# Depthwise 3x3 convolutions of a vision model: from nine diagonal matmuls to three stacked-row matmuls per 32-channel strip

## The chip, the cores and the metric

The kernel runs on one core of one Trainium2 chip. The metric is the device time of one execution in microseconds (us), the median of three runs. The engines are called PE (TensorE), DVE (VectorE), ACT (ScalarE), POOL (GpSimd) and SP (SyncE, which here only issues DMAs).

## The reference

The input is `x`, 8 images of 56x56 pixels and 192 channels, in f32. Four residual layers follow one another, each on the group-normalized (32 groups) result of the one before:

```python
x = x + L0(gn(x))   # gated Toeplitz mixing along rows and columns, 576 inner channels
x = x + L1(gn(x))   # shifted 7x7 window attention, 6 heads
x = x + L2(gn(x))   # depthwise 3x3 convolution, 192 channels, zero padding, bias
x = x + L3(gn(x))   # in_proj to 2x384, depthwise 3x3 convolution of 384 channels, SiLU,
                    # selective scans of 16 states in 4 directions, layer norm, gate, out_proj
```

A depthwise convolution treats every channel by itself: output pixel (h, w) of channel c is the sum over dy, dx of w[dy, dx, c] times the pixel (h+dy-1, w+dx-1) of the same channel, with zeros outside the image. The change concerns the two depthwise convolutions, in L2 (called conv2 below) and in L3 (conv3).

## The kernel before, in words

Channels lie on the partitions, pixels along the free axis, and an image is taken in seven chunks of 8 rows (448 pixels, `CH`). The program has three phases.

1. `products` and `toeplitz` for images 0 to 3 (layer L0's mixing).
2. The `front` of image 0, and between its pieces `products` and `toeplitz` of images 4 to 7. What is left of these when the front is done is run after it. A scheduler of the framework orders this phase.
3. The scans of all eight images, and between them the fronts of images 1 to 7. The order of this phase is written out by the kernel itself.

`front(b)` is a chain of five stages: `gate` (L0's end), `attention` (L1), `conv2` (L2), `inner` (in_proj and conv3 of L3), `steps` (the scan's coefficients). Each is a Python generator that yields between pieces of work. All of them work in one SBUF buffer, `slab`, which each stage carves up anew.

The scan goes over 224 chunks (8 images, 4 directions, 7 chunks), each with 3 channel blocks `d` and 8 pairs of states `k`: 5376 steps. One step multiplies on POOL (`ring`, L1007), exponentiates on ACT (L1024), scans on DVE (L1033), multiplies by C on POOL or DVE in turn (`hc`, L1039), and adds up on PE with two matmuls by the identity (`ps_y`, L1054). `hc` has four buffers. SP loads `bm` and `cm`, broadcast rows, some eight steps ahead.

In the loop over the steps a planner (`Parts`) keeps a modelled clock for each engine. After each step it lets the front run on as long as the modelled work fits before the next scans; the costs come from `Meter`, which gives a PE instruction 0.04 us plus 1.25 ns a column. The order that results is fixed when the program is built, and each engine runs its list in order. A front must have made a chunk's coefficients before that chunk's scan comes up, else the planner runs the front alone until it has.

conv2 before: for each chunk `load_x` brings 10 rows of each 96-channel half (one row above and below), DVE normalizes them into a tile `xp` with a zero column at each side (L736), and nine matmuls add the nine taps (L749). Each has a 96x96 diagonal matrix of one tap as its weights (made once, kept in DRAM as `dg2_d`) and a shifted view of `xp` as moving data. DVE adds bias and residual (L758) and takes statistics. After each three matmuls the generator yields.

conv3 before: for each of the three 128-channel blocks, in_proj writes its convolution half into a padded image `xp` in SBUF (58x58, L804) and the other half through `zt`, two buffers, to `zr_d` in DRAM (L801, L802). Then for each chunk nine matmuls with 128x128 diagonals (`dg3_d`) follow (L817), and ACT evicts (L826). SiLU, and a transposed copy, follow for the whole block, with stores of 1.5 MB each.

The front of image 0 and the first closing passage of a scan (`finish`, which norms, gates and projects) run through a metering helper, so their instructions have line L79 in the profile. (L0 to L3 above are layers; elsewhere L and a number is a line of the kernel.)

Of the kernel before, what the change touches and what calls it, by code (L numbers as in the profile page):

```python
# [38 lines left out]
SLAB, SLAB_F = 10048, 2688 + HALF  # L39
SLOT = NG * (CH + 1) + HALF  # L40
# [18 lines left out]
class MeteredEngine:  # L59
# [3 lines left out]
    def __getattr__(self, name):  # L63
# [3 lines left out]
        def call(*args, **kw):  # L67
            n, extra = 0, 0.0
            for v in list(args) + list(kw.values()):
                if hasattr(v, "shape") and (engine != "E" or n == 0):  # L70
                    m = 1
                    for s in v.shape[1:]:
                        m *= s
                    n = max(n, m)
            if name == "preload_act_table_set" or AF.Silu in args or AF.Softplus in args:
                extra = 1.28
            if name != "dma_start":
                self.meter.log.append((engine, base + each * n + extra))
            return f(*args, **kw)  # L79
# [5 lines left out]
def model(ctx: ExitStack, tc: tile.TileContext, a: dict, out: bass.AP):  # L85
# [31 lines left out]
    dg2_d = dram.tile([CP, 2, 9, CP], F32, name="dg2_d")  # L117
    dg3_d = dram.tile([128, ND, 9, 128], F32, name="dg3_d")
# [178 lines left out]
    with (  # L297
# [66 lines left out]
        cw2, cw3, dg2, dg3 = carve(slab, 128, (2, 9), (ND, 9), (2, 9, CP), (ND, 9, 128))  # L364
        nc.sync.dma_start(out=cw2[:CP], in_=a["cw2"])
        nc.sync.dma_start(out=cw3, in_=a["cw3"])
        for t in range(9):
            for k in range(2):
                nc.vector.tensor_scalar_mul(dg2[:CP, k, t, :], ident[:CP, :CP], cw2[:CP, k, t : t + 1])
            for d in range(ND):  # L370
                nc.vector.tensor_scalar_mul(dg3[:, d, t, :], ident, cw3[:, d, t : t + 1])
        nc.sync.dma_start(out=dg2_d, in_=dg2[:CP])
        nc.sync.dma_start(out=dg3_d, in_=dg3)
# [316 lines left out]
        def conv2(b):  # L690

            dg, xh, xp, xo = carve(slab, CP, (2, 9, CP), (2, 2, 10, W), (2, 2, 10, W + 2), (2, 2, CH))
            nc.sync.dma_start(out=dg, in_=dg2_d)

            def span(j):

                return max(8 * j - 1, 0), min(8 * j + 9, H)

            def load_x(j):
                r0, r1 = span(j)  # L700
                at = r0 - (8 * j - 1)
                for k in range(2):
                    nc.sync.dma_start(
                        out=xh[:, j % 2, k, at : at + r1 - r0, :],
                        in_=x2_d[b][k * CP : (k + 1) * CP, r0 * W : r1 * W].rearrange("p (h w) -> p h w", w=W),
                    )


            def load_all(j):
                nc.sync.dma_start(out=xo[:, j % 2], in_=blocks(x2_d[b])[:, :, j * CH : (j + 1) * CH])  # L710

            load_all(0)
            load_all(1)
            yield 0, 0, 6.0
            for j in range(NCH):
                for k in range(2):
                    nc.vector.bn_stats(out=st[:, k, j, :], in_=xo[:, j % 2, k, :])
                    yield 0, 0, 2.0
                if j + 2 < NCH:
                    load_all(j + 2)  # L720
            load_x(0)
            yield from group_norm(NCH)
            for u in range(2):
                for k in range(2):
                    nc.scalar.activation(xp[:, u, k, :, 0 : W + 2 : W + 1], ident[:CP, 0:20].rearrange("p (h u) -> p h u", u=2), AF.Copy, scale=0.0)
            nc.scalar.activation(xp[:, 0, :, 0, :], ident[:CP, : 2 * W + 4].rearrange("p (k w) -> p k w", k=2), AF.Copy, scale=0.0)
            for j in range(NCH):
                r0, r1 = span(j)
                at = r0 - (8 * j - 1)
                u = j % 2  # L730
                if j + 1 < NCH:
                    load_x(j + 1)
                else:
                    nc.scalar.activation(xp[:, u, :, 9, :], ident[:CP, : 2 * W + 4].rearrange("p (k w) -> p k w", k=2), AF.Copy, scale=0.0)
                for k in range(2):
                    nc.vector.tensor_scalar(  # L736
                        xp[:, u, k, at : at + r1 - r0, 1 : W + 1],
                        xh[:, u, k, at : at + r1 - r0, :],
                        mr[:, k, 0:1],
                        mr[:, k, 1:2],  # L740
                        ALU.subtract,
                        ALU.mult,
                    )
                for k in range(2):
                    yield 0, 1
                    p = bank()
                    for t in range(9):
                        dy, dx = divmod(t, 3)
                        nc.tensor.matmul(  # L749
                            p[:CP, :CH],  # L750
                            dg[:, k, t, :],
                            xp[:, u, k, dy : dy + 8, dx : dx + W],
                            start=t == 0,
                            stop=t == 8,
                        )
                        if t % 3 == 2:
                            yield 1, 0
                    nc.vector.scalar_tensor_tensor(  # L758
                        xo[:, u, k, :],
                        p[:CP, :CH],  # L760
                        cb2[:, k : k + 1],
                        xh[:, u, k, 1:9, :].rearrange("p h w -> p (h w)"),
                        ALU.add,
                        ALU.add,
                    )
                    nc.vector.bn_stats(out=st[:, k, j, :], in_=xo[:, u, k, :])
                nc.sync.dma_start(out=blocks(x3_d[b])[:, :, j * CH : (j + 1) * CH], in_=xo[:, u])
# [3 lines left out]
        def inner(b):  # L771

            w_in, x, zt, xp, xc = carve(slab, 128, (2, 2 * 128), (2, 2, CH), (2, CH), (H + 2, W + 2), (L,))
            dg = carve(slab[:, 512:], 128, (9, 128))[0]
            w_in, x = w_in[:CP], x[:CP]
            for d in range(ND):
# [10 lines left out]
                for e in (xp[:, 0 : H + 2 : H + 1, :], xp[:, :, 0 : W + 2 : W + 1]):  # L787
                    nc.scalar.activation(e, ident[:, :116].rearrange("p (u v) -> p u v", u=e.shape[1]), AF.Copy, scale=0.0)
                for j in range(NCH):
                    if j + 1 < NCH:  # L790
                        load_x(j + 1)
                    for u in range(2):
# [7 lines left out]
                        if u:  # L800
                            nc.scalar.activation(zt[:, j % 2, :], p[:, :CH], AF.Identity, bias=nb[:, 1:2])  # L801
                            nc.sync.dma_start(out=zr_d[b][:, d, j * CH : (j + 1) * CH], in_=zt[:, j % 2, :])  # L802
                        else:
                            nc.scalar.activation(  # L804
                                xp[:, 8 * j + 1 : 8 * j + 9, 1 : W + 1],
# [4 lines left out]
                nc.sync.dma_start(out=dg, in_=dg3_d[:, d])  # L810
                yield 0, 0, 6.0
                for j in range(NCH):
                    yield 0, 1
                    p = bank()
                    for t in range(9):
                        dy, dx = divmod(t, 3)
                        nc.tensor.matmul(  # L817
                            p[:, :CH],
                            dg[:, t, :],
                            xp[:, 8 * j + dy : 8 * j + dy + 8, dx : dx + W],  # L820
                            start=t == 0,
                            stop=t == 8,
# [547 lines left out]
```

## Time and profile before

| what | value |
|---|---|
| median of three runs | 21839.35 us (21826.98 to 21850.64) |
| the profiled execution, its own time | 21800.17 us |
| its span | 21798.4 us, 194536 instructions |
| PE, DVE, ACT, POOL busy | 84%, 73%, 56%, 69% of the span |
| conv2's matmuls (L749, images 1 to 7) | 1764 instructions, 725.1 us busy |
| conv3's matmuls (L817, images 1 to 7) | 2646 instructions, 1086.4 us busy |
| the scan's adding matmuls (L1054) | 21504 instructions, 9818.6 us busy |
| DMA | 3249.8 MB, mean 149 GB/s |

Busy shares are averages over three phases with different limits: POOL does next to nothing in the first 3.4 ms. An f32 matmul appears as two instructions. A group's mean is the time of one instruction from start to end, and neighbours overlap on PE, so busy time divided by the count says what one costs in a dense stretch.

### The profile page before, as it was taken

Reading aid. Unit: us, or ns where it says so; the run is one execution under the profiler, and the core shown is the slowest. Engines: PE = TensorE matmul, PEld = TensorE weight load, DVE = VectorE, ACT = ScalarE, POOL = GpSimd, SP = SyncE. Lnnn points to the kernel's source line nnn. Section 1 sums busy time; section 2 is a strip of 40 time slices with the busy share of each in tenths; the row PEclk is TensorE's granted clock in tenths of the full one; section 3 lists DMA queues with packets and bytes.
Section 4 is the critical chain, followed back from the end, with each engine's and each line's share of the span. In section 5 each row is a group of like instructions: output and inputs, shape, how many; then the busy total and the mean of one; then the engine's idle time right before and its main releaser. Section 6 shows DMA issues by size and latency. Waiting matters only on the chain. (4 is left out here: it accounts for less than half of the span.)

```text
span 21798.4 us, 194536 instructions
## 1 busy us (share of the span) xinstructions
PE 18274.4 (84%) x58396; PEld 9706.4 (45%) x58396; DVE 15858.5 (73%) x12604; ACT 12098.2 (56%) x28153; POOL 15084.9 (69%) x9175
## 2 busy tenths in 40 slices
PE   7978977888888989888888889888988888887777
PEld 4845654444443434444444434443444444343333
DVE  2122117996799768986799769976898589976998
ACT  3126114655666466755666566746675566656555
POOL 0000006887789778977788768976898678877998
PEclk9588868999999989998999989998999899998888
DMA  3931575444544455445644455345544464445443
GB/s 86 245 98 49 170 196 169 126 135 159 187 143 135 136 184 170 129 129 171 184 133 136 154 184 150 123 150 170 169 129 140 156 185 132 135 155 175 134 138 116
DMA packets 2419572, 3249.82 MB, mean 149 GB/s; under 512 B 917598, under 2 KB 2361024, under 8 KB 2387554
## 3 DMA queue, kind: packets, MB, share of 16 engines
q1 hardware_dynamic: 2398292, 3121.12, 47.5%
q0 software_dynamic: 15520, 116.14, 1.4%
q8 instruction: 463, 7.59, 0.1%
q14 instruction: 593, 4.86, 0.1%
q10 hardware_dynamic: 4704, 0.12, 0.0%
HBM read 2661.35 MB, written 575.48 MB: 148 GB/s over the span
## 5 line engine op out<-in xcount | busy, mean ns | idle before, releaser
L1007 POOL TENSOR_TENSOR ring<-du,bm 128x896 f32<-128x896 f32 x5376 | 9447.8, 1771 | 1983.9 <-ACT ring L1014 1937.8
L1054 PE MATMUL ps_y<-hc,ident_sb 128*128 128x448 f32 x21504 | 9818.6, 591 | 590.2 <-POOL hc L1039 573.3
L1024 ACT ACTIVATE ps_a<-delta,A_logs_sb 128x449 f32<-128x449 f32 x10752 | 6858.4, 638 | 331.5 <-DVE ring L1033 68.7
L1054 PEld LDWEIGHTS ps_y<-hc,ident_sb 128*128 128x128 f32 x21504 | 4271.5, 207 | 4640.8 <-issue 3494.9
L1033 DVE TENSOR_TENSOR_SCAN ps_a<-ps_a,ring 128x898 f32<-128x898 f32 x2688 | 5429.0, 2020 | 1062.5 <-ACT ring L1014 555.0
L1033 DVE TENSOR_TENSOR_SCAN ring<-ps_a,ring 128x898 f32<-128x898 f32 x2688 | 5423.0, 2017 | 420.4 <-ACT state L1046 177.3
L1039 POOL TENSOR_TENSOR hc<-ring,cm 128x896 f32<-128x896 f32 x2688 | 4758.0, 1770 | 860.9 <-DVE ring L1033 349.3
L1039 DVE TENSOR_TENSOR hc<-ps_a,cm 128x896 f32<-128x896 f32 x2688 | 2935.0, 1092 | 974.5 <-PE ps_y L1054 753.3
L1046 ACT COPY state<-ps_a 128x2 f32<-128x2 f32 x2687 | 425.3, 158 | 3254.0 <-DVE hc L1039 3250.0
L280 DVE COPY tzx<-ps_tz 112x448 f32<-112x448 f32 x432 | 269.8, 625 | 1389.9 <-PE ps_tz L274 1175.0
L274 PE MATMUL ps_tz<-tzx,tm 112*112 112x112 f32 x4608 | 1031.5, 403 | 257.6 <-DMA tm<-ext 233.0
L288 POOL DMA_DIRECT2D o<-tzx x192 | 97.3, 513 | 1653.6 <-DVE tzx L280 1318.7
L274 PEld LDWEIGHTS ps_tz<-tzx,tm 112*112 112x112 f32 x4608 | 1028.0, 319 | 295.2 <-issue 288.7
L817 PE MATMUL ps_f<-slab 128*128 128x448 f32 x2646 | 1086.4, 546 | 69.9 <-DMA slab<-dg_d 62.1
L1046 ACT COPY state<-ring 128x2 f32<-128x2 f32 x2688 | 504.9, 188 | 791.3 <-DVE ring L1033 778.4
L647 PE MATMUL ps_f<-ident_sb,slab 98*98 98x98 f32 x1344 | 336.5, 326 | 619.6 <-ACT slab L640 619.6
L749 PE MATMUL ps_f<-slab 96*96 96x448 f32 x1764 | 725.1, 547 | 47.7 <-DVE slab L736 47.7
L817 PEld LDWEIGHTS ps_f<-slab 128*128 128x128 f32 x2646 | 506.8, 192 | 560.5 <-issue 485.0
L79 PE MATMUL ps_f<-slab 96*96 96x448 f32 (+6 forms) x2306 | 731.2, 497 | 10.2 <-DMA slab<-x 4.9
L990 POOL TENSOR_TENSOR du<-delta,xcd 128x448 f32<-128x448 f32 x672 | 658.6, 980 | 23.6 <-DMA xcd<-xc 23.6
L647 PEld LDWEIGHTS ps_f<-ident_sb,slab 98*98 98x98 f32 x1344 | 203.9, 158 | 1033.7 <-ACT slab L640 814.6
L227 PE MATMUL ps_qv<-wqv,xn 96*128 96x384 f32 (+1 forms) x1200 | 527.0, 522 | 128.2 <-DVE xn L146 67.5
(218 smaller groups left out, 17070.7 us busy)
## 6 DMA issues: line engine op xcount, KB each, us to landing
bm<-bc SPq DMA_DIRECT2D x1792, 448.0 KB
cm<-bc SPq DMA_DIRECT2D x1792, 448.0 KB
xcd<-xc SPq DMA_DIRECT2D x840, 224.0 KB
dl<-slab SPq DMA_DIRECT2D x224, 672.0 KB
delta<-dl SPq DMA_DIRECT2D x224, 672.0 KB
tzx<-qv SPq DMA_DIRECT2D x192, 588.0 KB
o<-tzx POOLq DMA_DIRECT2D x192, 588.0 KB, 13.7
slab<-x SPq DMA_DIRECT2D x224, 336.0 KB
```

The lines of the kernel that those rows point to most:

```text
L79: return f(*args, **kw)
L274: nc.tensor.matmul(po[:, c, :], t[:, :, c2 + c], x[:, :, c1 + c2 + c], start=True, stop=True)
L647: nc.tensor.transpose(p[:PT_, e * PT_ : (e + 1) * PT_], S[:, 3 * g + e, :], ident[:PT_, :PT_])
L749: nc.tensor.matmul(p[:CP, :CH], dg[:, k, t, :], xp[:, u, k, dy : dy + 8, dx : dx + W], start=t == 0, stop=t == 8,)
L817: nc.tensor.matmul(p[:, :CH], dg[:, t, :], xp[:, 8 * j + dy : 8 * j + dy + 8, dx : dx + W], start=t == 0, stop=t == 8,)
L990: nc.gpsimd.tensor_mul(du[:, 0, :], deltas[i][:, d, 1 : CH + 1], xcs.pop((i, d)))
L1007: nc.gpsimd.tensor_mul(hs[:, :, tokens(i)[0]], dus[i, d].to_broadcast([128, NG, CH]), bms[i, k])
L1024: nc.scalar.activation(dA[:, n, :], deltas[i][:, d, at : at + CH + 1], AF.Exp, scale=negA[:, slot, d, c : c + 1])
L1033: nc.vector.tensor_tensor_scan(h, dA, hs, 0.0, ALU.mult, ALU.add)
L1039: (nc.gpsimd if on_pool(d, k) else nc.vector).tensor_mul(hc, h[:, :, tokens(i)[0]], cms[i, k])
L1046: nc.scalar.copy(states[i][:, d, NG * k : NG * k + NG], h[:, :, tokens(i)[2]])
L1054: nc.tensor.matmul(yps[i, d][:, :CH], ident, hcs[g][:, n, :], start=k + n == 0, stop=k + n == NP + NG - 2)
```

## The change

The convolution over dy moves into the contraction. Three copies of 32 channels, shifted by 0, 1 and 2 image rows, lie one above the other on 96 partitions. The weights of one dx are then a 96x32 matrix (three 32x32 diagonals), and one matmul yields 32 channels; three matmuls (dx) make up one 32-channel strip. A strip's output goes to its own 32 PSUM partitions[...]. A chunk takes 3 strips x 3 = 9 matmuls for a 96-channel half in conv2 as before, and 4 x 3 = 12 instead of 9 for a 128-channel block in conv3. All matmuls of a chunk are issued before the generator yields.

The shifted copies are made by DMA. The normalized input (conv2) and in_proj's output (conv3) are stored with a zero column at each side into padded images in DRAM (58x58, two for each convolution, used by images in turn); for each group three DMAs, one for each dy, load the rows from there into `xs`, two buffers. The top and bottom rows of the padded images are set to zero once, by ten DMAs on ACT's queue. In conv2 the normalization moves from DVE to ACT, the input is loaded once, without the neighbouring rows, into four buffers `xh`, and each loaded chunk is also the residual and the place of the result. In `inner` the padded image in SBUF is gone; `zt` has one buffer instead of two. The planner's model counts a matmul into 32 columns or fewer at a third of its columns.

```diff
+            if engine == "E" and args[0].shape[0] <= 32:
+                n /= 3
...
-    dg2_d = dram.tile([CP, 2, 9, CP], F32, name="dg2_d")
-    dg3_d = dram.tile([128, ND, 9, 128], F32, name="dg3_d")
+    dg2_d = dram.tile([CP, C // 32, 3, 32], F32, name="dg2_d")
+    dg3_d = dram.tile([CP, DI // 32, 3, 32], F32, name="dg3_d")
+    pad2_d, pad3_d = (
+        [dram.tile([n, (H + 2) * WP], F32, name=f"pad{m}_{q}") for q in range(2)] for m, n in ((2, C), (3, DI))
+    )
...
         def conv2(b):
-            dg, xh, xp, xo = carve(slab, CP, (2, 9, CP), (2, 2, 10, W), (2, 2, 10, W + 2), (2, 2, CH))
+            dg, xh, xn, xs = carve(slab, CP, (C // 32, 3, 32), (4, 2, CH), (2, 2, 8, WP), (2, 3, RUN))
...
+            def load_rows(n):
+                j, k = divmod(n, 2)
+                for dy in range(3):
+                    at = (8 * j + dy) * WP
+                    nc.sync.dma_start(
+                        out=xs[32 * dy : 32 * dy + 32, n % 2], in_=stacked[:, 3 * k : 3 * k + 3, at : at + RUN]
+                    )
+            def normal(j):
                 for k in range(2):
+                    nc.scalar.activation(
+                        xn[:, j % 2, k, :, 1 : W + 1],
+                        xh[:, j % 4, k, :].rearrange("p (h w) -> p h w", w=W),
+                        AF.Identity, scale=mr[:, k, 1:2], bias=vb[:, k : k + 1],
+                    )
+                at = (8 * j + 1) * WP
+                nc.sync.dma_start(out=blocks(pad)[:, :, at : at + RUN], in_=xn[:, j % 2].rearrange("p k h w -> p k (h w)"))
...
             for j in range(NCH):
+                if j + 2 < NCH:
+                    normal(j + 2)
                 for k in range(2):
+                    n = 2 * j + k
                     yield 0, 1
                     p = bank()
-                    for t in range(9):
-                        dy, dx = divmod(t, 3)
-                        nc.tensor.matmul(
-                            p[:CP, :CH],
-                            dg[:, k, t, :],
-                            xp[:, u, k, dy : dy + 8, dx : dx + W],
-                            start=t == 0, stop=t == 8,
-                        )
-                        if t % 3 == 2:
-                            yield 1, 0
+                    for dx in range(3):
+                        for g in range(3):
+                            nc.tensor.matmul(
+                                p[32 * g : 32 * g + 32, :CH],
+                                dg[:, 3 * k + g, dx, :],
+                                xs[:, n % 2, g].rearrange("p (h w) -> p h w", w=WP)[:, :, dx : dx + W],
+                                start=dx == 0, stop=dx == 2,
+                            )
+                    if n + 2 < 2 * NCH:
+                        load_rows(n + 2)
+                    yield 1, 0
+                    x = xh[:, j % 4, k, :]
+                    nc.vector.scalar_tensor_tensor(x, p[:CP, :CH], cb2[:, k : k + 1], x, ALU.add, ALU.add)
+                    nc.vector.bn_stats(out=st[:, k, j, :], in_=x)
+                nc.sync.dma_start(out=blocks(x3_d[b])[:, :, j * CH : (j + 1) * CH], in_=xh[:, j % 4])
+                if j + 4 < NCH:
+                    load_all(j + 4)
...
         def inner(b):
-            w_in, x, zt, xp, xc = carve(slab, 128, (2, 2 * 128), (2, 2, CH), (2, CH), (H + 2, W + 2), (L,))
+            xc, xT, own = carve(slab, 128, (L,), (L,), (SLAB - 2 * L,))
+            w_in, x, zt, xt = carve(own, 128, (2, 2 * 128), (2, 2, CH), (CH,), (2, 8, WP))
+            xs, dg = carve(own, CP, (2, 4, RUN))[0], carve(xT, CP, (4, 3, 32))[0]
...
+                            at = (8 * j + 1) * WP
+                            nc.sync.dma_start(
+                                out=pad[d * 128 : (d + 1) * 128, at : at + RUN],
+                                in_=xt[:, j % 2].rearrange("p h w -> p (h w)"),
+                            )
...
+                for j in range(2):
+                    load_rows(d, j)
+                yield 0, 0, 8.0
                 for j in range(NCH):
                     yield 0, 1
                     p = bank()
+                    for dx in range(3):
+                        for g in range(4):
+                            nc.tensor.matmul(
+                                p[32 * g : 32 * g + 32, :CH],
+                                dg[:, g, dx, :],
+                                xs[:, j % 2, g].rearrange("p (h w) -> p h w", w=WP)[:, :, dx : dx + W],
+                                start=dx == 0, stop=dx == 2,
+                            )
+                    if j + 2 < NCH:
+                        load_rows(d, j + 2)
+                    yield 1, 0
```

## The prediction

> **What bounds the kernel now.** I read the row of slices first. After the first 3.4 ms POOL jumps from 0 to 7 to 9 tenths and stays there: that is the scan, 5376 steps (I call one a pair: one scan, two adding matmuls of L1054), and beside it the "front" of images 1 to 7 is fed in. So the next view is the busy time by stretch: attention, conv2, the first conv3 block of image 1, and the end, where no front is left.
>
> ```profile
> core 0: us, PE busy (x) PEld busy (x) DVE busy (x) ACT busy (x) POOL busy (x), PEclk, DMA share, GB/s
> 3900.00:4600.00 700.00, 578.90 (x2100) 286.82 (x2099) 660.87 (x552) 500.51 (x1468) 630.93 (x378) 0.91 0.41 127
> 4677.00:4849.00 172.00, 161.96 (x424) 73.66 (x425) 146.00 (x116) 66.36 (x158) 123.31 (x74) 0.98 0.39 120
> 4916.00:4997.00 81.00, 78.05 (x208) 39.11 (x207) 58.07 (x37) 36.71 (x85) 61.54 (x38) 1.00 0.34 116
> 20100.00:21700.00 1600.00, 1161.01 (x2464) 521.93 (x2465) 1464.85 (x930) 847.06 (x1939) 1555.08 (x936) 0.87 0.42 136
> ```
>
> In attention VectorE is 94% busy, at the end POOL is 97% busy: there the convolutions could cost nothing. In the convolutions PE is 94 to 96% busy at full clock while DVE falls to 72% and POOL to 76%. The same stretches with the scans (L1033) alone give the rate:
>
> ```profile
> 3900.00:4600.00 700.00, 463.95 (x232) 0.91 0.41 127
> 4677.00:4849.00 172.00, 91.06 (x46) 0.98 0.39 120
> 4916.00:4997.00 81.00, 45.61 (x23) 1.00 0.34 116
> 20100.00:21700.00 1600.00, 1124.96 (x564) 0.87 0.42 136
> ```
>
> One pair takes 1600/564 = 2.84 us alone, 3.0 in attention, but 172/46 = 3.7 in conv2 and 81/23 = 3.5 in conv3 (4.0 in the second block of that image). PE's timeline inside conv3 shows why:
>
> ```profile
> 4935.80 2.42 PE L817 MATMUL ps_f<-slab 128*128 128x448 f32 x6
> 4938.06 1.67 PE L1054 MATMUL ps_y<-hc,ident_sb 128*128 128x448 f32 x4
> 4939.56 2.42 PE L817 MATMUL ps_f<-slab 128*128 128x448 f32 x6
> ```
>
> Three taps, one pair, three taps, without a gap: a period of 3.76 us, 0.376 us per instruction (each f32 matmul is two), 1.50 us per pair. PE is the bound here and nothing else.
>
> To price whole stages I laid the count of L1054 over time (10 us stretches) on PE's compiled order, which says between which pairs each front stage stands. Over the seven fronts: conv2 stands in 312 pairs and lasts 1178 us; conv3 in 447 pairs (21 blocks) and 2059 us. The 610 pairs after the last front take 1729 us, 2.834 each. What a stage costs beyond its pairs is then 1178 - 312 x 2.834 = **294 us** for conv2 and 2059 - 447 x 2.834 = **792 us** for conv3. These 1086 us are the stake; all other stages together carry some 2,040 us, which the change leaves.
>
> **What the Trainium skill says.** "TensorE: Matmul & The Clock Gate", Part 3 (packing small matmuls): outputs in different 32-column strips run at once; three strips of M=32, N=512 gave 2.38 times, four row strips 3.07 times. The trace has such strips in attention, with separate moving data each:
>
> ```profile
> 4014.04 0.54 PE L659 MATMUL ps_f<-slab 98*32 98x98 f32 x12
> ```
>
> Twelve instructions in 0.54 us, of which one alone lasts 0.25: (0.54 - 0.25)/11 = 26 ns each, where 98 columns at the rate above would take 82. So the overlap is real for f32, near 3 times. "DMA: Bandwidth & Descriptors", Anatomy of one DMA, puts a fixed cost of about 2 us on a transfer, mostly the receipt of the write (stated for the gpsimd path), and its Rules for kernel authors say that a DMA that reads what another wrote must wait for its semaphore. On the SP queue the trace agrees, a buffer's reload waiting for its store (335 KB): 105.3/39 = 2.7 us.
>
> ```profile
> SPq L438 <- DMA x<-slab: 105.3, 39, 4.5
> o<-tzx POOLq DMA_DIRECT2D x192, 588.0 KB, 13.7
> ext<-rpe_et POOLq DMA_DIRECT2D x2, 252.0 KB, 5.4
> ```
>
> **The change part by part.**
> *The order.* The kernel's own planner prices a strip at a third, and now emits a whole group (9 or 12 matmuls) between two pairs. In the compiled order conv2 stands in 14 pairs instead of 44.6, a conv3 block in 9.6 instead of 21.3. Gate and attention take some 80 pairs more over all fronts, for the same work, so at the base price. Fronts end at pair 4418 instead of 4766; 958 pairs instead of 610 run alone. Those pairs cost 2.834 us wherever they stand, so only the sums beyond the base change.
>
> *conv3, PE.* A group goes from 9 matmuls (18 x 0.376 = 6.8 us) to 12 in four strips: 24 x 0.376/3.07 = 2.9 us (2.3 if they overlap fully, 9.0 if not at all). A block is 7 x 2.9 + 9.6 x 1.5 = 34.7 us against 9.6 x 2.834 = 27.2: 7.5 beyond. The old block had 98 - 47.4 (126 instructions) - 21.3 x 1.5 = 18.6 us that are neither taps nor pairs (the finish of the scanned image, the load of dg); by pairs 8.4 remain. So 16 x 21 = 334 us where 792 stood: **-458**.
>
> *conv3, rows by DMA.* Each group's rows come in three DMAs (238 KB each, 713 together) that SP may issue only when PE has done the group two before, and SP is in order. From a group's end to the start of the next but one, PE has one group and two shares of pairs: 2.9 + 2 x 2.05 = 7.0 us. Three issues at some 0.4 us (SP's timeline: 0.32 to 0.55), then 2.7 for the receipt and about 2 for the bytes (densest stretch: 350 GB/s): 5.9. It fits, barely; cost nothing, and where the landing is longer, each us costs half a us per group, 74 us over 147 groups. What stands behind on SP are the bm and cm loads, due some six pairs (17 us) later; behind PE the adding matmuls, for which hc has four buffers.
>
> *conv2.* PE: 18 x 0.376/2.38 = 2.8 us a group, 14 x (2.8 + 1.5) = 60 us. But SP goes through a chain in each of 7 iterations: nine DMAs (3.6 us), the row load with dy=2 waits for the padded rows just written (2.7, less two issues: 1.9), the store of x3 for the eviction on DVE (0.68 + 0.5, and 1.5 behind a scan), the reload of that buffer for the store (2.7): 10.9 us, 76 in all, against 14 x 2.834 = 40. So 36 x 7 = 255 where 294 stood, plus the first round trip (normalize, store, load) which the planner puts at 6 us and I at 11: 5 x 7. **About 0**; bounds -150 (PE alone) and +250 (DMA waits twice as long). Traffic is 15 MB plus 4 of bm and cm in 76 us, 250 GB/s, heavy but below 350.
>
> *Normalizing moves* from DVE (14 x 0.88 us an image) to ACT (14 x 0.63). ACT is 39% busy there and covers it; uncovered 9 us an image.
>
> *zt has one buffer.* ACT's next z eviction waits for the store before it. The stores leave every 6.0 us in in_proj and land in 3 to 5: I take 30 us over 147, and up to 150. The padded stores (21 an image, 0.35 us of SP each) lie beside.
>
> *After the convolutions* a block's bulk stores (1.5 MB each) make PE wait for the next weights. Where PE used to arrive late itself (before steps, 4 pairs became 10.6) that wait shows: 9 x 7, **+65**.
>
> *First image and set-up.* There Toeplitz products follow conv2 and run at about 95 us for 96 matmuls, and at 75 once alone; they start some 85 us later in PE's new order, and 408 instead of 144 are left at the end. Net **+15**, -80 to +100. The set-up trades 45 DVE scalings and 2.4 MB of stores for 6, 0.2 MB and ten small ACT stores: 10 us either way.
>
> Sum: -458 + 0 + 65 + 30 + 15 = about **-350 us**, on a profiled execution of 21800.2 us (span 21798.4). The median of the three runs shown is 21839.4, 0.2% above it; I apply the difference there: 21,490 us. About 0.2%, 44 us, is what a measurement of this kernel can tell from no change.
>
> **The rivals.**
> 1. *The round trips hide* (25%). conv2 runs at PE's 60 us (-150), the 8.4 us of other work per conv3 block lies beside (-177), zt and the late stall cost nothing (-80): 21,080. For it: ACT and DVE have room in these stages. Against: SP's chain is serial by its waits.
> 2. *SP's round trips take PE's place as the bound* (11%). One mechanism: rows that are late on a landing of 9 us after issue instead of 4.7. conv3 then costs (10.2 - 7.0)/2 = 1.6 us more a group, 235 in all; conv2's iteration, with two such waits, 16.5 us instead of 10.9: +275. Together 22,000, slower. It decides from a landing of about 8 us. For it: 252 KB took 5.4 us and 588 KB 13.7 on POOL's queue. Against: SP's 2.7 us receipt.
> 3. *The strips do not overlap at 448 columns* (3%): 9.0 and 6.8 us a group, 7 x 9.0 + 14.4 = 77 us a block and 14 x 8.3 = 115 in conv2, 22,500. L659 speaks against it.
> 4. *Nothing that shows* (6%): the gain in conv3 is eaten by half the delay of rival 2.
>
> **How the numbers follow.** My case has 55%, its own range 21,300 to 21,680. Faster by over 0.2% holds my case and rival 1: 0.80; within 0.2%: 0.06; slower: 0.14. The range reaches to 21,120, near rival 1's number, and to 21,850, the no-change case; rivals 2 and 3 and the lower part of rival 1 lie outside.
>
> **What would show it.** Right: 12 strip matmuls in about 3 us on PE's timeline, near 10 pairs and 40 us per conv3 block, conv2 some 75 us with PE waiting for rows, a tail of some 950 pairs at 2.83 us, 20 us more of PE idle before steps. Wrong: PE waiting for "slab<-pad" in conv3 by more than 1 us a group, a pair rate below 3.6 us in conv2, attention or gate slower per pair than 3.0 and 3.3, ACT waiting for zr, or a first scan later than 3.5 ms.

## The result, and the profile after

| | median us (range) | ratio to before, 95% interval |
|---|---|---|
| before, beside the runs of after | 21836.05 | 1 |
| after | 21631.75 (21617.34 to 21674.55) | 0.991 (0.9897 to 0.9922) |

The change saves 204 us, 0.9%; 350 were forecast. The profiled execution of after has a span of 21636.7 us.

The busy time by stretch of after: attention of image 1, conv2 and the first conv3 block of that image, each from its first group (the matmuls of one chunk) to its last, attention of image 7 and the end without fronts. The columns are those of the header line.

```profile
core 0: us, PE busy (x) PEld busy (x) DVE busy (x) ACT busy (x) POOL busy (x), PEclk, DMA share, GB/s
3900.00:4600.00 700.00, 576.33 (x2085) 284.51 (x2083) 663.20 (x555) 503.12 (x1480) 632.06 (x378) 0.92 0.41 129
4723.00:4795.00 72.00, 63.04 (x309) 20.38 (x309) 53.44 (x50) 26.65 (x59) 41.51 (x26) 0.88 0.70 193
4862.70:4905.10 42.40, 39.38 (x209) 13.75 (x209) 24.47 (x16) 16.07 (x36) 27.43 (x17) 0.84 0.85 225
17150.00:18010.00 860.00, 703.82 (x2482) 360.43 (x2481) 762.86 (x637) 577.88 (x1655) 744.97 (x449) 0.90 0.44 134
18950.00:21550.00 2600.00, 1891.69 (x4116) 868.22 (x4114) 2355.52 (x1503) 1378.13 (x3150) 2514.93 (x1515) 0.87 0.42 135
```

The same stretches with the scans (now L1085) alone, and last the attention of image 7 in the kernel before (its L1033):

```profile
core 0: us, DVE busy (x), PEclk, DMA share, GB/s
3900.00:4600.00 700.00, 464.56 (x233) 0.92 0.41 129
4723.00:4795.00 72.00, 29.41 (x15) 0.88 0.70 193
4862.70:4905.10 42.40, 19.00 (x10) 0.84 0.85 225
17150.00:18010.00 860.00, 527.29 (x264) 0.90 0.44 134
18950.00:21550.00 2600.00, 1803.07 (x902) 0.87 0.42 135
...
18140.00:18900.00 760.00, 508.52 (x254) 0.93 0.41 127
```

This conv3 block lasts 42 us where it lasted 81, and conv2 72 where it lasted 172. Over all seven fronts, from first group to last, a conv3 block takes 39.1 us (before 89.4) and conv2 84.0 (before 171.2). But the two stretches now hold 10 and 15 pairs, at 4.2 and 4.8 us each, and PE is still busy for 0.93 and 0.88 of the time. Image 1's attention keeps its rate, 700/233 = 3.00 us a pair. Image 7's does not: 860/264 = 3.26, where before it was 760/254 = 2.99. That is new, and it is where part of the gain went.

PE's timeline in conv3 and in conv2. The bracket is idle time and what ended it.

```profile
4871.54 2.46 PE L869 MATMUL ps_f<-slab 96*32 96x448 f32 x24
4873.93 1.77 PE L1106 MATMUL ps_y<-hc,ident_sb 128*128 128x448 f32 x4
...
4893.86 4.71 PE L869 MATMUL ps_f<-slab 96*32 96x448 f32 x24 [2.87 <-DMA slab<-pad]
```

```profile
4740.03 2.46 PE L780 MATMUL ps_f<-slab 96*32 96x448 f32 x18
4742.42 1.77 PE L1106 MATMUL ps_y<-hc,ident_sb 128*128 128x448 f32 x4
...
4761.09 4.70 PE L780 MATMUL ps_f<-slab 96*32 96x448 f32 x18 [6.89 <-DMA slab<-pad]
```

A group takes 2.39 us from its start to the next work, with 18 instructions or with 24. At the prediction's 0.376 us of one instruction that is an overlap of 18 x 0.376/2.39 = 2.8 and 24 x 0.376/2.39 = 3.8 times.

The finish of a scanned chunk (from here a passage; 56 in all) left the Mamba branch in the new order. In the compiled order of PE 12.7 of them stood in in_proj and 19.1 in conv3; after, none does, and 21.9 stand in the gate and 11.7 in the attention. The groups of their instructions in image 7's attention, in the stretch shown above:

```profile
L993 PE MATMUL ps_f<-slab_f,w_out_sb 128*96 128x224 f32 x120 | 30.4, 395 | 21.6 <-POOL slab_f L988 21.6
L959 PE MATMUL ps_f<-ysum,ones 128*128 128x448 f32 x30 | 15.3, 657 | 1.1 <-ACT slab L670 1.1
L959 PE MATMUL ps_f<-slab_f,ones 128*128 128x224 f32 x60 | 14.6, 382 | 5.8 <-ACT slab_f L971 5.8
L981 POOL TENSOR_TENSOR slab_f<-slab_f 128x672 f32<-128x672 f32 x10 | 13.8, 1380 | 22.2 <-ACT slab_f L977 19.5 <-issue 1.9 <-POOL hc L1091 0.8
```

L959 on ysum runs six instructions a passage: 30/6 = five passages, each with (30.4 + 15.3 + 14.6)/5 = 12.1 us of PE.

The table lays all runs beside one another, by the prediction's method: what each part of the seven fronts costs beyond its pairs at 2.834 us, its surcharge, in the profiled execution. "conv2" reaches from attention's end to in_proj, "Mamba" from in_proj to the first matmul of the steps. Passages are given in the order gate and attention / Mamba / steps / tail; the tail is what follows the last front. The 56th passage is the first one, which has the helper's line. "First scan" is the time at which the scan's sums begin on PE, in us. The parts' borders are good to some tens of us: read from the traces between the parts' first and last instructions, the changes from before to after are +449, -4, -538 and -141 us, where the table has +424, 0, -585 and -75.

| kernel | ratio | gate, attention | conv2 | Mamba | steps | passages | first scan |
|---|---|---|---|---|---|---|---|
| before | 1 | 715 | 442 | 1366 | 600 | 0/32/16/7 | 3420 |
| after | 0.991 | 1139 | 442 | 781 | 525 | 34/0/7/14 | 3455 |
| nofin_before | 0.969 | 751 | 450 | 919 | 397 | none | 3437 |
| nofin_after | 0.9591 | 714 | 437 | 773 | 411 | none | 3455 |
| lock44 | 0.9887 | 764 | 444 | 833 | 790 | 0/13/34/8 | 3444 |
| fullprice | 0.9768 | 693 | 222 | 1034 | 598 | 0/32/16/7 | 3446 |
| conv2only | 0.9918 | 889 | 432 | 968 | 751 | 10/8/28/9 | 3335 |
| conv3only | 0.9952 | 920 | 475 | 828 | 747 | 13/4/27/11 | 3474 |
| split_price | 0.984 | 931 | 225 | 814 | 760 | 14/3/27/11 | 3505 |
| xh5 | 0.9896 | 1158 | 393 | 795 | 534 | 34/0/7/14 | 3446 |
| conv2_full | 0.9863 | 708 | 238 | 1311 | 553 | 0/32/16/7 | 3410 |
| conv3_full | 0.9893 | 707 | 447 | 1172 | 565 | 0/33/16/7 | 3434 |
| price_1_5 | 0.9782 | 884 | 233 | 671 | 837 | 6/13/28/8 | 3477 |
| nofin_full | 0.946 | 756 | 236 | 615 | 374 | none | 3470 |

The medians of before beside the three sets of runs were 21803.99, 21854.17 and 21814.50 us, so I compare ratios.

### The profile page after: what moved, and what is told of

It reads as the page before. It is cut to its first block, busy times and chain, and to the rows that moved or that the text cites. A ratio compares the mean times of both kernels' runs of the same rounds, so it can differ in the third digit from the quotient of the medians.

```text
span 21636.7 us, 198667 instructions
## 1 busy us (share of the span) xinstructions
PE 17516.4 (81%) x59404; PEld 9109.9 (42%) x59404; DVE 15781.2 (73%) x12469; ACT 12150.2 (56%) x28249; POOL 15086.4 (70%) x9176
## 5 line engine op out<-in xcount | busy, mean ns | idle before, releaser
L1106 PE MATMUL ps_y<-hc,ident_sb 128*128 128x448 f32 x21504 | 10046.0, 605 | 966.8 <-POOL hc L1091 957.4
L1106 PEld LDWEIGHTS ps_y<-hc,ident_sb 128*128 128x128 f32 x21504 | 4331.0, 211 | 5336.0 <-issue 3600.1
L1085 DVE TENSOR_TENSOR_SCAN ps_a<-ps_a,ring 128x898 f32<-128x898 f32 x2688 | 5429.7, 2020 | 954.6 <-ACT ring L1066 485.6
L1085 DVE TENSOR_TENSOR_SCAN ring<-ps_a,ring 128x898 f32<-128x898 f32 x2688 | 5422.1, 2017 | 488.2 <-ACT state L1098 180.6
L83 PE MATMUL ps_f<-slab 96*32 96x448 f32 (+7 forms) x2432 | 604.2, 569 | 71.2 <-DMA slab<-pad 51.5
L1066 ACT COPY ring<-state 128x6 f32<-128x6 f32 x1536 | 292.8, 191 | 629.0 <-POOL ring L1059 627.7
L503 PE MATMUL ps_f<-ident_sb,slab 112*96 112x112 f32 x4704 | 529.1, 267 | 101.0 <-DVE slab L511 53.5
L503 PEld LDWEIGHTS ps_f<-ident_sb,slab 112*96 112x96 f32 x4704 | 506.6, 169 | 240.3 <-issue 105.5
```

What stands on the lines that cost most here:

```text
L503: nc.tensor.matmul(p[:CP, t * TT : (t + 1) * TT], ot[:, n % 2, i, t, c % 2 * CP : c % 2 * CP + CP], ident[:TT, :TT], start=i == 0, stop=i ...
L1085: nc.vector.tensor_tensor_scan(h, dA, hs, 0.0, ALU.mult, ALU.add)
L1106: nc.tensor.matmul(yps[i, d][:, :CH], ident, hcs[g][:, n, :], start=k + n == 0, stop=k + n == NP + NG - 2)
```

## The experiments

**Both kernels without the scan's closing work.** `finish` only copies x3 to the output; the layer norm, gate and out_proj are missing. The same edit in both:

```diff
         def finish(b, j):
-            yc, _, sq, rs, x3 = carve(slab_f, 128, (ND, CH), (HALF,), (ND, CH // 2), (CH // 2,), (2, CH // 2))
+            x3 = carve(slab_f, CP, (2, CH // 2))[0]
...
                 nc.sync.dma_start(out=x3, in_=blocks(x3_d[b])[:, :, tok])
-                nc.vector.tensor_add(x3, x3, p[:CP, :CH].rearrange("p (m n) -> p m n", m=2))
                 nc.sync.dma_start(out=blocks(out[b])[:, :, tok], in_=x3)
```

> The kernel before with the closing passages of the scan left out (no layer norm, gate or out_proj: each of the 56 passages only copies its piece of x3 to the output). Theory F: these passages stood mostly under conv3, in_proj and steps, where they cost little (about 5 us each, 240 in all), so this runs at about 21,550 us. Theory G (the passages cost the same wherever they stand, some 12 us): about 21,150.

> The changed kernel with the closing passages of the scan left out in the same way. Theory F (the change lets the fronts drift against the images, so that the passages fall into gate and attention, where they cost 11 to 15 us each): 21,080 us, so about 470 us below the kernel before without them, more than twice the 204 between the two kernels with them; gate and attention take 433 and 850 us in every front. Theory G (gate and attention slow down for another reason, a lower PE clock or busier DMA queues): the distance stays near 200 us, and gate stays at 470 to 530 us in the later fronts.

Measured: 21125.99 us (0.969, 0.9677 to 0.9704) and 20908.73 (0.9591, 0.9578 to 0.9604). Before loses 678 us, 12.1 a passage; after loses (0.991 - 0.9591) x 21804 = 696, 12.4 a passage. So on the average of its places a passage costs the same in both kernels. The theory that passages were cheap beside conv3 and dear beside gate and attention falls: 217 us remain between the two kernels without any passage, as many as with them. What does follow: gate and attention of after without passages (714) are as fast as before's (751). So their extra 424 us is the work that the order put there. A lower granted clock is not the reason: its mean is 0.862 in after and 0.889 in before, but it stays at 0.862 without the passages, too.

**The next front held back for 44 pairs,** so that passages are done in the steps instead:

```diff
-                if ahead_of not in parts.clients and b_next < B:
+                if ahead_of not in parts.clients and b_next < B and g >= 672 * (b_next - 1) + 44:
```

> The changed kernel, but a front may start only 44 steps after its predecessor image's scan has begun, so that no closing passage meets gate or attention (34 fall into steps, 9 into conv3, 4 into in_proj, 8 after the last front). Theory F: gate back to 433 us and attention to 835 to 855 in every front. If the passages are dear only in gate and attention, 250 to 400 us faster than the changed kernel (21,230 to 21,380). If they are cheap only where PE alone is the bound, they cost as much in steps and the time stays within 100 us of 21,630. Theory G: gate and attention stay slow.

Measured: 21555.25 us, 0.9887 (0.9873 to 0.99), some 50 us better than after, with intervals that still touch. The 250 to 400 us of the first branch did not come; the time is within the second's 100 us. Gate and attention fall from 1139 to 764, steps rise from 525 to 790. Most of what left the one came back in the other; moving passages is not the way to the missing gain.

**The planner's third taken back.** The convolutions are those of after; only the model that orders the program prices a strip's matmul in full again:

```diff
-            if engine == "E" and args[0].shape[0] <= 32:
-                n /= 3
```

> The changed kernel, but the planner counts a strip matmul at its full columns again, so that a group of 9 or 12 stands in two to three steps instead of one: conv2 in 38 steps, a conv3 block in 20, fronts as long as before and the passages where they were. Theory F: PE has room in the convolutions (7 x 2.4 + 20 x 1.5 = 47 us of work in 56 us of steps), the rows have time to land, and gate and attention are at 433 and 835 us: 21,200 to 21,450. Rival: the gain lies in the shorter fronts, which this takes back: 21,650 to 21,850.

Measured: 21292.55 us, 0.9768 (0.9755 to 0.9781), 511 us under before, the fastest kernel of the study that computes everything, and some 310 us better than after by the ratios. The theory's range holds, and the rival falls. The order has front starts and passages like before's; that the places of the passages are not what pays is shown by the last experiment. PE's timeline in its conv2:

```profile
4735.59 2.46 PE L778 MATMUL ps_f<-slab 96*32 96x448 f32 x18
4737.98 3.27 PE L1104 MATMUL ps_y<-hc,ident_sb 128*128 128x448 f32 x8
4742.36 1.77 PE L1104 MATMUL ps_y<-hc,ident_sb 128*128 128x448 f32 x4 [1.11 <-POOL hc L1089]
4744.06 2.46 PE L778 MATMUL ps_f<-slab 96*32 96x448 f32 x18
```

Between groups there are two or three pairs now, and PE waits for POOL: the scan itself is the limit again, not PE. The waits of PE for rows, total, times and longest, of after and of fullprice (conv2, then conv3):

```profile
PE ps_f L780 <- DMA slab<-pad: 151.4, 42, 11.9
PE ps_f L869 <- DMA slab<-pad: 181.2, 38, 10.0
```

```profile
PE ps_f L778 <- DMA slab<-pad: 85.1, 31, 8.8
PE ps_f L867 <- DMA slab<-pad: 69.1, 20, 8.3
```

For conv2 this nearly closes the account. In after one image has 14 pairs and 14 groups: PE's own work is 14 x (2.39 + 1.70) = 57 us. Of its waits, 16 us an image stand behind the first group, and groups that run slowly after a wait (the last section) cost 8 us more: together 81 of the 84 us that conv2 lasts. In fullprice an image has 38 pairs: 38 x 2.834 = 108 us at the base rate, and 9 us of waits behind the first group, together 117; conv2 lasts 118.8. Beside two or three pairs a group is nearly covered by the scan; beside one it isn't.

**Each convolution alone, with the third.** The other one is that of the kernel before, with its tiles and weights; what stays of the change is, in one case, `conv2`, `dg2_d` and `pad2_d`, in the other `inner`, `dg3_d` and `pad3_d`:

```diff
-        for pads in (pad2_d, pad3_d):
+        for pads in (pad2_d,):
```

is conv2only's set-up; conv3only has `(pad3_d,)` there.

> Only the 96-channel convolution is changed; the Mamba branch's is that of the kernel before. Theory (conv2's half brings nothing by itself): its block falls from 168 to about 76 us but runs beside 14 instead of 45 step pairs, surcharge 294 to about 257, and the stretch before it and the first image take about 75 us more: 21,780 to 21,850 on a base of 21,804. Rival (the front of the kernel before, 696 pairs, is longer than the 672 pairs of an image, so that its end is forced into the scan; any shortening that takes it under 672 frees that): the front is 666 pairs here, the third conv3 block of fronts 4 to 7 loses its extra 58 us each, and the kernel falls by 150 to 230 us to 21,570 to 21,650.

> Only the Mamba branch's convolution is changed (rows from the padded DRAM copy, 4 strips); the 96-channel convolution is that of the kernel before. Theory (the gain is the conv3 block's): the block's span falls from 98.0 to about 32 us, the passages leave it (13 in the gate, 27 in the steps, 3 in conv3 by the order, at about 12 us each wherever they stand), so that 7 x 3 blocks give back what was neither passage nor base, about 312 - 60 = 250 us, less about 130 us that the queued work between conv3 and the steps costs more: 120 to 200 us under the kernel before, 21,600 to 21,690 on a base of 21,804. Rival (the gain comes from the new lengths of both, which let the fronts follow without delay): each half alone gives nearly all of it, and this one stands at 21,600 like the other. Rival (work is only moved): within 50 us of the kernel before.

Measured: conv2only 21663.11 us, 0.9918 (0.9902 to 0.9935); conv3only 21739.41, 0.9952 (0.9935 to 0.9969). My theory fell for conv2: I gave it nothing and it brings nearly as much as the whole change, though its own surcharge (432, before 442) doesn't move. The rival's number came, and its mark is there. In before, the front of 696 pairs doesn't fit the 672 of an image, and from image 4 on the third conv3 block is squeezed. The scans in the second and third block of image 4's front, of before:

```profile
12332.00:12466.00 134.00, 64.01 (x33) 0.91 0.53 176
12535.00:12676.00 141.00, 34.87 (x18) 0.82 0.41 139
```

These stretches begin in the blocks and reach past their ends. From first tap to last, the second block takes 85 us for 21 pairs, the third 96 for 18. PE's timeline of before behind the third shows one more cost: no pair runs while the block's store and reload go through.

```profile
12648.92 4.26 PE L866 MATMUL ps_f<-slab 128*128 128x448 f32 x6 [30.87 <-DMA slab<-xc]
```

In conv2only the front has 662 to 672 pairs. The third block of the same image takes 91 us for 24 pairs there, and its stretch holds 36:

```profile
12100.00:12245.00 145.00, 72.10 (x36) 0.91 0.54 181
```

Taking the passages off at 12 us each, Mamba goes from 1366 - 32 x 12 = 982 to 968 - 8 x 12 = 872 with an unchanged convolution. The first scan starts 85 us earlier as well. I did not find out why it starts between 3335 and 3505 us in these kernels. conv3only met none of the ranges; it stays 15 us short of its theory's by the ratio, and its interval reaches into it. Its Mamba stretch falls by 538 to 828, passages included, but 205 and 147 us come back in gate, attention and steps, where the passages went.

**The price split:** conv2's matmuls in full, conv3's at a third.

```diff
-            if engine == "E" and args[0].shape[0] <= 32:
+            if engine == "E" and args[0].shape[0] <= 32 and self.meter.cut:
...
+                    meter.cut = False
```

The last line stands ahead of conv2's matmuls; ahead of conv3's the flag is True.

> The changed kernel, with the planner's third of the price kept for conv3's strip matmuls and the full price for conv2's. In the order conv2 then has 267 pairs (98), conv3 204 (201), and the finish passages go to the steps (27) and the gate (14), none to the attention. Theory (the wide price pays because conv2's groups stand a step or more apart, so that rows land, SP's round trips and the x3 store are covered): conv2's surcharge falls from 257 to about 95 and the stretch before it by 45, 21,370 to 21,430 on a base of 21,804. Rival (it pays in conv3, or by where the passages go): 21,550 to 21,620, no better than the changed kernel or lock44.

Measured: 21494.58 us, 0.984 (0.9826 to 0.9855). It lies between the two theories' ranges. In place the theory is right: conv2's stretch falls from 442 to 225, the block itself from 257 to 86 (by the traces, from first group to last, from 305 to 77). In all it gains 0.7%, 153 us, on after, by the medians. The profiled executions, from which the table comes, differ by 111 us: of conv2's 217, 60 come back in the other parts (gate and attention -208, Mamba +33, steps +235) and 50 in the first scan. Half of fullprice's distance to after comes from conv2.

**Five x buffers in conv2 instead of four:** the reload no longer waits for the store of the chunk before it. (Each `j % 4` of `xh` becomes `j % 5`.)

```diff
-            dg, xh, xn, xs = carve(slab, CP, (C // 32, 3, 32), (4, 2, CH), (2, 2, 8, WP), (2, 3, RUN))
+            dg, xh, xn, xs = carve(slab, CP, (C // 32, 3, 32), (5, 2, CH), (2, 2, 8, WP), (2, 3, RUN))
```

> The changed kernel with five instead of four x buffers in conv2, so that the load of the rows four steps on doesn't wait for the store of the present ones; the order on TensorE is the same. Theory (SP's chain of round trips, store then reload then rows, sets conv2's pace): conv2 falls from 76 to about 60 us per image, about 100 us in all, 21,500 on a base where the changed kernel is at 21,608. Rival (TensorE itself and the step pairs between set it: 14 periods of 4.1 us and the rows' landing): under 40 us, 21,570 to 21,610.

Measured: 21619.95 us, 0.9896 (0.9881 to 0.991), against 0.991 with overlapping intervals. SP's wait for the store was real in after (total, times, longest):

```profile
SPq L717 <- DMA x<-slab: 131.3, 31, 9.3
```

It is gone with five buffers, and conv2 falls only from 84.0 to 76.8 us an image. The rival holds: SP's chain through the store is not what sets conv2's pace.

**Each convolution alone, at full price,** so that the order stays that of the kernel before. The edit is that of fullprice, made in conv2only and in conv3only.

> Only the 96-channel convolution is changed, and the planner prices its matmuls in full: the order of everything else is nearly that of the kernel before (front starts at pairs 0, 695, 1387, 2078, 2755, 3426, 4098; passages 8 in proj, 23 in conv3, 16 in steps, 7 in the tail; the block beside 266 pairs, before 312). Theory (at one order, what the engines save stays saved): conv2's surcharge falls from 294 to about 90, the start before the scan by up to 85: ratio 0.987 to 0.991. Rival (the end of fronts 4 to 7 is forced at 672 pairs an image, so that the saved time turns into nothing): 0.995 to 1.0, no better than conv2only's 0.9918.

> Only the Mamba branch's convolution is changed, priced in full: the order is that of the kernel before but for a few pairs (front starts 0, 701, 1398, 2082, 2754, 3426, 4098; passages 12.6 in proj, 19.9 in conv3, 15.6 in steps, 7 in the tail; conv3 beside 417 pairs, before 447). Theory (at one order the saving shows): conv3's surcharge falls from 792 to about 310, of which some 200 to 240 come back between the blocks (conv3 to steps, to proj, proj to conv3) and up to 50 before the scan: ratio 0.985 to 0.989, clearly under conv3only's 0.9952, and together with conv2_full the 0.977 of full price. Rival (the passages in conv3 cost it what the convolution saves): 0.994 to 0.998.

Measured: 21526.57 us, 0.9863 (0.9848 to 0.9878), and 21584.93, 0.9893 (0.9876 to 0.9909). Both ratios lie just outside their theories' ranges, the first with a little more gain and the second with a little less, and both intervals reach into them. Both rivals fall. The two savings, 1.37% and 1.07%, make 2.44%, and fullprice has 2.32%. At the order of before the halves add up. With the third each is worth less: 0.82% and 0.48%.

**Two thirds for conv3, full for conv2,** with the `cut` of the split price as a divisor:

```diff
-                n /= 3
+                n /= self.meter.cut
```

`cut` is 1.0 in conv2 and 1.5 in `inner`.

> The changed kernel with conv2's matmuls at the full price and conv3's at two thirds: fronts start exactly 672 pairs apart, so that none is forced; passages 28 in steps, 10 in conv3, 6 in the gate, 8 in the tail. Theory (what pays is the width of the convolution blocks): between the split price and the full price, ratio 0.978 to 0.983. Rival (forced fronts cost the full-price order something, and one that just fits does better): under 0.9755.

Measured: 21339.95 us, 0.9782 (0.9767 to 0.9796): the theory's range, not told apart from fullprice. Fronts that fit (672 pairs) bring nothing over fullprice's 690: 671 for Mamba instead of 1034, but 837 for the steps instead of 598 and 884 for gate and attention instead of 693. The long wait isn't gone either; PE's wait at the steps' first matmul for the block's stored and reloaded result, first of before, then of price_1_5 (total, times, longest):

```profile
PE ps_f L866 <- DMA slab<-xc: 165.0, 7, 31.3
```

```profile
PE ps_f L920 <- DMA slab<-xc: 205.2, 7, 29.7
```

So no gain from fitting into 672 pairs is seen here. But the price of conv3 changed together with the fit, so a gain and a loss could hide each other. That conv2only gains by the fit is seen only in its blocks: what of its 191 us that explains stays open.

**Full price without the passages:** both edits together, so that `finish` only copies, as above.

> Full price, with the finish passages' arithmetic left out (x3 is copied to the output in its place). Theory (a passage costs about 12 us wherever it stands, and full price gains through conv2's and conv3's own waits): the distance to the full-price kernel is again 56 x 12 = 670, ratio 0.944 to 0.949, about 0.012 to 0.015 under the changed kernel without passages (0.9591). Rival (full price gains because passages beside conv3's strips are cheap, those in the gate and the attention dear): the distance is 500 or less, ratio 0.953 to 0.959.

Measured: 20636.39 us, 0.946 (0.9446 to 0.9474). The distance to fullprice is (0.9768 - 0.946) x 21814 = 672 us, 12.0 a passage, in a third order. The rival (cheap beside the strips) falls again. And without a passage full price still leads by 1.31%, 286 us: its gain over after is not where passages stand.

## Why the prediction was right, and where not

- **What bounds.** Right: PE in the convolutions. After the change it still does in conv2, because the pairs went with the groups: 57 of 84 us are PE's own at full clock.
- **conv3 on PE.** 2.9 us a group forecast, 2.39 measured. 34.7 + 8.4 us a block forecast, 39.1 measured from first group to last. The sum is nearly right with another make-up: PE's own work is 7 x 2.39 + 9.6 x 1.70 = 33.0 us, and the rest is mostly waits for rows and the slow groups after them. The prediction's count by pairs gives 31.7, because it leaves out the first and the last group. "The Trainium skill", "TensorE: Matmul & The Clock Gate", Part 3, gave 2.38 for three strips and 3.07 for four row strips; for these f32 strips of 448 columns the traces show 2.8 and 3.8.
- **conv2.** 76 us and a surcharge of 255 forecast; 76.3 and 257 measured by the same count, 84.0 and 305 from first group to last (before 309). That conv2 brings nothing is right, the make-up isn't: I had SP's chain of 10.9 us an iteration and PE hidden under it. The account is 57 us of PE, 16 of waiting for rows and 8 of slow groups, and with one link of the chain taken out (xh5) only 7 us go. The 2.7 us that I read as the receipt of a store are only what was left of it when SP came to wait.
- **The step that failed: "gate and attention take some 80 pairs more, for the same work, so at the base price".** They take 424 us more beyond the base. In the same sum, the 18.6 us of other work in a conv3 block were let shrink by pairs to 8.4, some 214 us over 21 blocks. A large part of that work was passages, 12 us each by the three pairs of runs, and work with an amount of its own goes where the order puts it. By stretch: Mamba -585 where I had -458 + 65 = -393; gate and attention +424 where I had 0; steps -75 for 0; the first scan +35 for +15. These make -201, and the tail, where 14 passages stand instead of 7, adds some 38: -163, as the profiled executions differ (21800.17 and 21638.53 us; the medians differ by 204). I looked at which stage lost pairs and not at which work stood in the pairs. With 32 passages at 12 us taken off, Mamba falls only from 982 to 781. That the whole still came out within the range is in part luck: the passages that came into gate and attention had left Mamba, so that Mamba's gain, too small by 192 us in my sum, made up for part of the 424; and the range was 730 us wide.
- **The wait before the steps.** Forecast +65 us; it went the other way. PE's wait at the steps' first matmul for the block's stored and reloaded result was 165.0 us in before and is 75.0 in after.
- **zt's one buffer.** Forecast 30 us; ACT waited 51.7 us for stores of z in seven fronts. What of it reached the end was not tried.
- **Rivals.** No sign of rival 3. Rows are late, as in rival 2: PE's 181 us of waiting for them in conv3 are 1.2 us a group over 147 groups, over the 1 us that I had named as a sign. But some 136 of them stand before the first groups of the 21 blocks, 6.5 us each, and 0.4 us before each other group. The pace inside a block held. What I had put at nothing is the first round trip of a block (store the padded rows, load them): without the passages, the time between in_proj and conv3 costs 51 us more beyond its pairs in after than in before, and conv3 itself 179 less. The gain that rival 1 gave conv2 (150 us) is there in fullprice (its stretch falls by 220), but by the wider order and not by shorter round trips.
- **What I had not seen at all:** that the price in the planner's model was part of the change with an effect of its own, against it. The third is close to the truth for PE (2.72 us modelled for a conv3 group, 2.39 measured) and still the worse price: it lets nearly every group stand beside one pair or a little more, where neither PE nor the rows' landing is covered by the scan. At before's price the same instructions save 511 us instead of 204.
- **What would prove it wrong** named attention or gate slower per pair than 3.0 and 3.3. By the traces attention went from 3.00 to 3.09 us a pair and the gate, from the steps before it to attention, from 3.38 to 3.65: that was the sign. Of the signs that it was right, the groups came (2.46 us), the pairs of a conv3 block (9.8) and its 40 us, and the tail (957 pairs, though at 2.88 us with its passages).

Open: why the first scan's start moves, which engine makes a passage cost 12 us (PE's 12.1 is only the nearest row), and how Mamba's stretch falls by 55 us (by the traces 112) in conv2_full, where nothing in it was changed.

## What to carry to other kernels

Where a planner orders the program by modelled costs, a change of price is a second change: run the new instructions once at the old order before judging them. When a stage shrinks, ask for every piece of other work that stood in it where it will stand next, and charge it there. And in this kernel a group of short matmuls was hidden only where enough of the limiting engine's work stood between it and the next one; a nearly correct price for one engine said nothing about the time that its operands take to land.

## What the runs showed of the hardware that I had not expected

- f32 matmuls into three or four 32-column strips overlap almost fully: 18 and 24 instructions both take 2.46 us, so the fourth strip is free.
- A group that follows a long idle stretch of PE takes up to twice as long, and the trace shows half the clock while it runs. The two slow groups shown in the section on the profile after, which follow 2.87 and 6.89 us of waiting, as stretches of PE (the number before the last two is the granted clock):

```profile
core 0: us, PE busy (x), PEclk, DMA share, GB/s
4893.86:4898.57 4.71, 4.71 (x25) 0.50 1.07 315
4761.09:4765.80 4.71, 4.71 (x19) 0.50 0.57 136
```

"The Trainium skill", "TensorE: Matmul & The Clock Gate", Part 1, has the clock at half after an idle window of about 3.4 us. In after, all 45 groups that waited 4 us or more were slow (3.8 us at least), and of the 185 that waited less than 2 us none took more than 3.1. Between the two there is no fixed limit: a wait of 2.43 us was followed by a group of 4.16 us, one of 2.79 by a group at full speed:

```profile
11417.48 2.46 PE L780 MATMUL ps_f<-slab 96*32 96x448 f32 x18 [2.79 <-DMA slab<-pad]
```

Rows that land late cost PE twice, once waiting and once at the slow clock: what the groups of after take beyond 2.46 us adds up to 54 us in conv2 and 63 in conv3.
